# One reduce for both heads' maxima, and broadcast maxima copied into the score banks, in a fused FFN and attention kernel

## The chip, the cores and the metric

The kernel runs on one core of a Trainium2 chip. The metric is the device time of one execution, in microseconds (us), as the median of several runs. Five engines of the core work side by side, each on its own queue in program order: TensorE (PE, with its weight loads PEld), VectorE (DVE), ScalarE (ACT), GpSimd (POOL) and SyncE (SP), which here issues all DMAs.

## The reference

A "macaron" layer on x of shape 4 x 1024 x 128: half an FFN, attention, half an FFN, each on a layer norm of x.

```python
x = x + 0.5 * ffn(layernorm(x))
x = x + attn(layernorm(x))
x = x + 0.5 * ffn(layernorm(x))
```

The FFN is a mixture of 8 experts of width 128 with a router. The attention has 16 heads of 64 dimensions; queries, keys and values come from 64-dimensional latents, queries and keys get a rotary embedding:

```python
scores = jnp.einsum('bhqd,bhkd->bhqk', q, k) * scale      # scale = 1/8
attn = jax.nn.softmax(scores, axis=-1)
out = jnp.einsum('bhqk,bhkd->bhqd', attn, v)
out = out.transpose(0, 2, 1, 3).reshape(b, s, H * DH)
out = out @ w_out.T + residual
```

## The kernel before

The order of all instructions on every engine is written out by hand; there is no scheduler. Lists of closures (`self.at(group, fn, place)`) are run by `run_later(group, place)` at named places of the loop, and `step(...)` takes pieces of background work (layer norms, the latents of the next batch, the second router) as room allows.

The first FFN takes about the first 220 us, the second the last 150. In between, attention runs in 64 units (`for U in range(NUNIT)`). A unit is one batch, one pair of heads and 512 queries (half of the 1024), and it has 8 slots, one for each chunk of 128 keys. The two heads of a pair lie in partitions 0 to 63 and 64 to 127, so the matmuls of the two heads with 64 rows each use different halves of the array. `rows(0)` and `rows(1)` yield each head's matmuls, and the loop zips them, one of each head at a time.

What a unit computes, in TensorE's order:

- **Scores and maxima.** Per slot and head, four matmuls into one PSUM bank (`score`, L938): key by query as high x high, high x low and low x high parts, and a matmul of one row, `one_row` by `maxr`, which adds minus the row maximum of each query. ScalarE then takes the exponential into `p` (L942), and POOL adds the p of the slots into `acc` (L954). The 16 results of a unit go round six banks: four of `psS`, `psC`, `psX`. Among them stand the maxima of a later unit (`passA`): per head and for 128 queries by 512 keys, one matmul of the high parts into that head's bank `psA[hh]` (L912) and at once a VectorE reduce of that bank (L913). There are 8 such steps per head in a unit. `MAXIMA` holds at which positions among the 32 score matmuls of each head six of them stand: 2, 8, 13, 19, 24, 29 for head 0 and 0, 5, 11, 16, 21, 27 for head 1; the last two follow among the side work. `AHEAD = 15` slots lie between a score and the maxima computed beside it.
- **Side work** (`self.halves`): the output projection of an earlier unit (`outp`, L997) into banks `bankO` and the rotary embedding's matmuls (L797) into `rope_banks`, for a later batch.
- **Denominators** of the unit before (`den`, L974): four column sums of `acc` by a matmul with ones, into `psS[3]`, copied out by ScalarE and written to DRAM as `d1`; a transposing load brings them back as `dT` (L982), and VectorE takes the reciprocal for the projection's scaling (L993, L1012).
- **Values** (`values`, L962): 32 matmuls of p with the latent keys into `psC`, then a ScalarE copy to `osb` (L965).

After the side work VectorE has the rotary steps (L810 to L823) and the two additions of the projection to X (L1006), one at place "end" and one at "late".

When the last of a unit's 16 maxima is done, a small reduce (L917) combines them to `m8` [128, 8], negated. `max_row`, at place "mid" of the same unit, writes it to DRAM (`d`) and loads it back transposed into `maxr` as one row per head. All these DMAs stand on SP's queue, in order with the rotary stores (`qs`, `ks`), the latents' loads (`C_l`) and the loads of QT and KT, 16 of them for every two units. A DMA whose data is not ready holds the queue.

Of the kernel before, what the change touches and what calls it, by code (L numbers as in the profile page):

```python
# [10 lines left out]
F32 = mybir.dt.float32  # L11
# [13 lines left out]
LOWER = 0.5 - float(np.log(4.0 / 3.0))  # L25
UPPER = 0.5
CENTER = 1.0 / float(np.e)
AHEAD = 15
NSLOT = B * 128
NGRP = NSLOT // 4  # L30
NUNIT = NSLOT // 8
PBUFS = 10
MAXIMA = ((2, 8, 13, 19, 24, 29), (0, 5, 11, 16, 21, 27))
OTHER, VECTOR, PE, NEVER, SCALAR, POOL = 0, 1, 2, 3, 4, 5
NROPE = 9
ACTS = (4, 6, 7)
SWITCH, HOLD = 49, 49
FAR = 8
WLAG, GS, GD = 4, 17, 22
RATE0, RATE1, RATE2, RATE3 = 0.8, 2.8, 2.6, 1.6  # L40
# [7 lines left out]
class Kernel:  # L48
# [10 lines left out]
    def setup(self):  # L59
# [5 lines left out]
        self.prep = pool("prep", 1)  # L65

        bank = lambda name: pool(name, 1, space=PSUM).tile([128, 512], F32, name=name)
        self.psA, self.psS, self.psC, self.psX = [bank(f"ps_a{i}") for i in range(2)], [bank(f"ps_s{i}") for i in range(4)], bank("psc"), bank("psx")
        self.rest, self.nrest, self.slot, self.bankO = self.psA, 0, -NSLOT, None
        self.rope_banks = self.psA  # L70

# [25 lines left out]
        for t in self.maxr:  # L97
            nc.gpsimd.memset(self.f(t), 0.0)

        self.table = const.tile([128, 3, S], F32, name="table")  # L100
        self.rt = self.prep.tile([128, 4, 512], F32, name="rt")
        self.wr = const.tile([128, 2, 16], F32R, name="wr")
# [798 lines left out]
    def passA(self, a, hh):  # L901

        nc = self.nc
        U, i = divmod(a, 8)
        P, half = divmod(U, 2)
        qb, kk = divmod(i, 2)
        m = self.m_of.setdefault(U, [])
        if not m:
            m += [self.ms.tile([128, 2, 4, 2], F32, name="m"), 0]
        q0 = half * 512 + qb * 128  # L910
        r = slice(64 * hh, 64 * hh + 64)
        nc.tensor.matmul(self.psA[hh], self.QT[P % 3][r, 0, q0:q0 + 128], self.KT[P % 3][r, 0, kk * 512:kk * 512 + 512], start=True, stop=True)  # L912
        nc.vector.tensor_reduce(m[0][:, hh, qb, kk:kk + 1], self.psA[hh], AX.X, ALU.max)  # L913
        m[1] += 1
        if m[1] == 16:
            m8 = self.ms.tile([128, 8], F32R, name="m8")
            nc.vector.tensor_reduce(m8, self.m_of.pop(U)[0].rearrange("p h q k -> p (h q) k"), AX.X, ALU.max, negate=True)  # L917
            self.at(self.group, lambda: self.max_row(U, m8), "mid")

    def max_row(self, U, m):  # L920
        nc = self.nc
        d = self.dram.tile([128, 8], F32, name=f"d3_{U % 4}")
        self.dma(out=d, in_=m)
        self.dma(out=self.maxr[U % 2][0:128:64, :].rearrange("h (q p) -> h q p", p=128), in_=d.rearrange("p (h q) -> h q p", h=2))

    def score(self, s, hh, k):


        nc = self.nc
        U, c = divmod(s, 8)  # L930
        P, half = divmod(U, 2)
        qs = slice(half * 512, half * 512 + 512)
        ks = slice(c * 128, c * 128 + 128)
        r = slice(64 * hh, 64 * hh + 64)
        Q, K = self.QT[P % 3], self.KT[P % 3]
        ps = (self.psS + [self.psC, self.psX])[(2 * (s % 8) + hh) % 6]
        w, x = ((K[r, 0, ks], Q[r, 0, qs]), (K[r, 0, ks], Q[r, 1, qs]), (K[r, 1, ks], Q[r, 0, qs]), (self.one_row[r, :], self.maxr[U % 2][r, :]))[k]
        nc.tensor.matmul(ps, w, x, start=k == 0, stop=k == 3)  # L938
        if k == 3:
            if hh == 0:  # L940
                self.p_of[s] = self.pp.tile([128, 2, 512], F32, name="p")
            nc.scalar.activation(self.p_of[s][:, hh, :], ps, AF.Exp, scale=0.125)  # L942
            if hh == 1:
                self.accumulate(s)

    def accumulate(self, s):
# [20 lines left out]
    def den(self, U):  # L967

        nc = self.nc
        pd = self.psS[3]  # L970
        parts = [self.p_of[8 * U + c] for c in range(8 - direct(U), 8)] + [self.acc_of[U]]
        for k, part in enumerate(parts):
            for n in range(4):
                nc.tensor.matmul(pd[32 * n:32 * n + 32, 0:256], self.ones, part[:, n // 2, 256 * (n % 2):256 * (n % 2) + 256], start=k == 0, stop=k == len(parts) - 1)  # L974
        dsb = self.op1.tile([128, 256], F32, name="dsb")
        nc.scalar.copy(dsb, pd[:, 0:256])
        dT = self.ms.tile([128, 8], F32, name="dT")

        d1 = self.dram.tile([4, 256], F32, name=f"d1_{U % 4}")
        nc.sync.dma_start(out=d1, in_=dsb[0:128:32, :])  # L980
        g = 2 * U + 4
        self.at(g + (U == NUNIT - 1), lambda: nc.sync.dma_start(out=dT, in_=d1.rearrange("(h x) (y p) -> p (h x y)", x=2, p=128)), "mid")  # L982
        self.at(g + (2 if U == NUNIT - 1 else 1), lambda: self.outp(U, self.osb_of.pop(U), dT), "side")

    def outp(self, U, osb, dT):


        nc = self.nc
        P, half = divmod(U, 2)
        b, j = divmod(P, 8)  # L990
        po = self.bankO or self.psA
        rT = self.ms.tile([128, 8], F32, name="rT")
        nc.vector.reciprocal(rT, dT)  # L993

        def mm(i, hh):
            r = slice(64 * hh, 64 * hh + 64)
            nc.tensor.matmul(po[hh][:, i * 128:(i + 1) * 128], osb[r, i * 128:(i + 1) * 128], self.G[r, j, :], start=True, stop=True)  # L997

        for hh in range(2):
            self.halves[hh] += [lambda i=i, hh=hh: mm(i, hh) for i in range(4)]  # L1000

        def add(hh):

            t0 = b * TPB + 4 * half
            x = self.X[:, t0:t0 + 4, :]
            nc.vector.tensor_tensor(x, po[hh].rearrange("p (t d) -> p t d", t=4), x, ALU.add)  # L1006

        def scale():
            for hh in range(2):
                for i in range(4):  # L1010
                    c = slice(i * 128, (i + 1) * 128)
                    nc.scalar.activation(po[hh][:, c], po[hh][:, c], AF.Identity, scale=rT[:, 4 * hh + i:4 * hh + i + 1])  # L1012

        self.at(self.group, scale, "scale")
        self.at(self.group, lambda: add(1))
        self.at(self.group, lambda: add(0), "late")

    def run(self):
        nc, tc = self.nc, self.tc
# [39 lines left out]
        with ExitStack() as ctx:  # L1059
# [20 lines left out]
            def bg1(n, point):  # L1080
# [9 lines left out]
                if point == 2 and n >= 64 - AHEAD:  # L1090
                    self.group = (n - 64) // 4
                    for hh in range(2):
                        self.passA(n - 64 + AHEAD, hh)
                    if n % 4 in (1, 3):
                        self.run_later(self.group, ("mid", "end")[n % 4 // 2])
                if point < 3:
                    return
                if n == FAR:
# [24 lines left out]
        for _ in streams[2].pop() if streams[2] else ():  # L1123
            pass
        assert not (streams[0] or streams[2])
        self.rest, self.rope_banks, self.bankO = [self.psX, self.psS[3]], self.psS[1:3], [self.psX, self.psS[0]]
        flows, needs, blocks = [], {}, list(range(1, B))
        self.attending = True

# [27 lines left out]
        for U in range(NUNIT):  # L1157
# [4 lines left out]

            def rows(hh):
                maxima = lambda i: self.passA(s0 + AHEAD + i, hh) if s0 + AHEAD + i < NSLOT else None
                for n in range(32):
                    if n in MAXIMA[hh]:
                        yield lambda n=n: maxima(MAXIMA[hh].index(n))
                    yield lambda n=n: self.score(s0 + n // 4, hh, n % 4)
                if hh == 1:
                    yield lambda: maxima(6)  # L1170
                for n, fn in enumerate(side[hh]):
                    if hh == 0 and n == 2:
                        yield lambda: maxima(6)
                    yield fn
                if hh == 0 and len(side[hh]) < 3:
                    yield lambda: maxima(6)
                yield lambda: maxima(7)

            for n, pair in enumerate(zip_longest(rows(0), rows(1))):
                for fn in pair:  # L1180
# [2 lines left out]
                if n == 0:  # L1183
                    while self.deferred:
                        self.deferred.pop(0)()
                    for _ in range(2):
                        step(POOL, OTHER)
                if n == 9:
                    self.run_later(2 * U, "mid")
                    rope(U, "high")  # L1190
# [10 lines left out]
                    self.run_later(2 * U, "end")  # L1201
                if n == 26:
                    self.run_later(2 * U + 1, "mid")
                if n == 32:
                    self.run_later(2 * U + 1, "side")
                    rope(U, "side")
            self.halves = [[], []]
# [7 lines left out]
            rope(U, "vector")  # L1215
            self.run_later(2 * U + 1, "end")
            rope(U, "low")
            self.run_later(2 * U + 1, "late")
            rope(U, "end")
            for k in range(8):  # L1220
                self.values(s0 + k)
                if k % 2 == 0 or U < 8:
                    step(SCALAR, OTHER, *((VECTOR,) if k in (2, 3, 6, 7) else ()))
# [13 lines left out]
        with ExitStack() as ctx:  # L1237
# [6 lines left out]
            g = self.ffn_pre(self.prep, (6, 7), x_of, self.wts2[:, 3].rearrange("p e t -> p t e"), rows=3)  # L1244

            def bg2(n):
                for place in ("mid", "side", "scale", "end", "late"):
                    self.run_later(NGRP + 1 + n, place)
                    self.both()
                if n >= GS:  # L1250
# [59 lines left out]
```

## Time and profile before

| | |
|---|---|
| median of 3 runs | 1622.16 us (1620.22 to 1623.82) |
| the profiled execution | 1621.56 us, its profiled span 1619.7 us |
| granted TensorE clock, mean | 0.995 |
| first and last copy of a unit's output (L965) | 240.5 and 1457.4 us, 64 of them |
| DMA | 212.27 MB, 131 GB/s in the mean |

The page of the profile gives the busy time of each engine, a row per resource over 40 equal slices of the span, the chain of work that ended last, and groups of instructions: line, engine, operation, output and inputs by tile, shape, count, then busy time and mean ns of one, then the idle time of the engine just before them and what ended it. Timelines list instructions by start and length, merged where they follow each other. A line of the table of waits gives who waited for whom, the sum in us, how often, and the longest.

TensorE's matmuls are pipelined: the length of one is longer than the distance to the next.

### The profile page before, as it was taken

Reading aid. Unit: us, or ns where it says so; the run is one execution under the profiler, and the core shown is the slowest. Engines: PE = TensorE matmul, PEld = TensorE weight load, DVE = VectorE, ACT = ScalarE, POOL = GpSimd, SP = SyncE. Lnnn points to the kernel's source line nnn. Section 1 sums busy time; section 2 is a strip of 40 time slices with the busy share of each in tenths; the row PEclk is TensorE's granted clock in tenths of the full one; section 3 lists DMA queues with packets and bytes.
Section 4 is the critical chain, followed back from the end, with each engine's and each line's share of the span. In section 5 each row is a group of like instructions: output and inputs, shape, how many; then the busy total and the mean of one; then the engine's idle time right before and its main releaser. Section 6 shows DMA issues by size and latency. Waiting matters only on the chain.

```text
span 1619.7 us, 31073 instructions
## 1 busy us (share of the span) xinstructions
PE 1570.5 (97%) x10924; PEld 1054.0 (65%) x10924; DVE 1298.5 (80%) x2308; ACT 1115.2 (69%) x2488; POOL 1378.8 (85%) x820
## 2 busy tenths in 40 slices
PE   7998999999999999999999999999999999999998
PEld 5876766666666666566666666666666666556776
DVE  6566678898888889988888898889888866616897
ACT  4675667768777777777777777777677676665554
POOL 5678889989888889988989998989998898994676
PEclk9999999999999999999999999999999999999999
DMA  7025565565555555555555555655665532025543
GB/s 230 1 66 157 156 170 144 133 156 132 144 132 131 153 149 138 150 139 138 132 144 144 133 142 135 166 151 139 152 153 137 130 93 55 2 93 148 140 132 102
DMA packets 241148, 212.27 MB, mean 131 GB/s; under 512 B 157664, under 2 KB 170592, under 8 KB 240224
## 3 DMA queue, kind: packets, MB, share of 16 engines
q1 hardware_dynamic: 240992, 210.28, 50.0%
q8 instruction: 87, 1.43, 0.4%
q14 instruction: 69, 0.57, 0.1%
HBM read 130.39 MB, written 79.82 MB: 130 GB/s over the span
## 4 chain that ended last, share of the span: by engine, by line
PE 82%; DVE 6%; ACT 4%; POOL 3%; DMA 2%; issue 2%; SPq 1%; POOLq 0%; DVEq 0%; ACTq 0%
PE psc L962 25%; PE ps_s L938 21%; PE ps_a L912 8%; PE psc L938 4%; PE ps_s L463 3%; PE psx L938 3%; PE ps_s L543 3%; PE ps_s L797 2%; PE ps_s L997 2%; PE ps_s L974 2%; DVE m L913 2%; PE psx L498 2%; PE psc L434 1%; PE psx L997 1%; PE psc L543 1%
## 5 line engine op out<-in xcount | busy, mean ns | idle before, releaser
L954 POOL TENSOR_TENSOR acc<-acc,p 128x1024 f32<-128x1024 f32 x381 | 907.0, 2381 | 29.8
L913 DVE TENSOR_REDUCE m<-ps_a 128x1 f32<-128x512 f32 x1024 | 671.2, 685 | 161.9 <-PE ps_a L912 138.5
L942 ACT ACTIVATE p<-ps_s 128x512 f32<-128x512 f32 x768 | 411.5, 601 | 66.5 <-PE ps_s L938 42.7
L962 PE MATMUL psc<-p,ckn 128*64 128x512 f32 x2048 | 453.6, 595 | 0.0
L938 PE MATMUL ps_s<-QT,KT 64*128 64x512 f32 x2304 | 420.1, 394 | 0.3 <-DVE C_a L718 0.3
L912 PE MATMUL ps_a<-KT,QT 64*128 64x512 f32 x1024 | 390.1, 413 | 7.6 <-DVE m L913 5.8
L962 PEld LDWEIGHTS psc<-p,ckn 128*64 128x64 f32 x2048 | 141.4, 137 | 282.0 <-issue 282.0
L938 PEld LDWEIGHTS ps_s<-QT,KT 64*128 64x128 f32 x2304 | 284.3, 184 | 57.4 <-DVE X L1006 17.0
L954 POOL TENSOR_TENSOR acc<-p 128x1024 f32<-128x1024 f32 x64 | 153.8, 2403 | 86.8 <-ACT p L942 84.5
L912 PEld LDWEIGHTS ps_a<-KT,QT 64*128 64x128 f32 x1024 | 174.1, 184 | 43.4 <-DVE m L913 17.3
L938 PE MATMUL ps_s<-maxr,one_row 64*128 64x512 f32 x768 | 194.5, 392 | 0.0
L820 ACT CAST hi_r<-ps_s 128x512 fp32r<-128x512 f32 x110 | 64.5, 587 | 122.7 <-DVE ps_s L815 119.5
L938 PE MATMUL psx<-QT,KT 64*128 64x512 f32 x384 | 119.1, 390 | 0.0
L965 ACT COPY osb<-psc 128x512 f32<-128x512 f32 x64 | 37.3, 583 | 111.5 <-PE psc L962 111.5
L938 PE MATMUL psc<-QT,KT 64*128 64x512 f32 x384 | 109.2, 390 | 0.0
L938 PEld LDWEIGHTS ps_s<-maxr,one_row 64*128 64x128 f32 x768 | 102.4, 184 | 10.0
L551 POOL TENSOR_TENSOR p<-eo,p 128x512 fp32r<-128x512 f32 x42 | 62.7, 1499 | 41.5 <-ACT p L550 32.6
L1012 ACT ACTIVATE psx<-psx,rT 128x128 f32<-128x128 f32 x248 | 85.2, 344 | 17.5 <-ACT p L942 11.5
L447 POOL TENSOR_TENSOR X<-X,dtmp 128x512 f32<-128x512 f32 x54 | 69.2, 1281 | 31.7 <-ACT dtmp L446 30.6
L1012 ACT ACTIVATE ps_s<-ps_s,rT 128x128 f32<-128x128 f32 x248 | 84.3, 340 | 6.0
L942 ACT ACTIVATE p<-psc 128x512 f32<-128x512 f32 x128 | 77.4, 605 | 6.7 <-PE ps_a L912 3.3
L942 ACT ACTIVATE p<-psx 128x512 f32<-128x512 f32 x128 | 77.9, 608 | 0.0
(268 smaller groups left out, 2664.0 us busy)
## 6 DMA issues: line engine op xcount, KB each, us to landing
C_l<-cs SPq DMA_DIRECT2D x128, 256.0 KB
QT<-qs SPq DMA_DIRECT2D x256, 128.0 KB
KT<-ks SPq DMA_DIRECT2D x256, 128.0 KB
qs<-hi_r SPq DMA_DIRECT2D x32, 512.0 KB
qs<-eo SPq DMA_DIRECT2D x32, 512.0 KB
ks<-hi_r SPq DMA_DIRECT2D x32, 512.0 KB
ks<-eo SPq DMA_DIRECT2D x32, 512.0 KB
rt<-wt SPq DMA_DIRECT2D x52, 256.0 KB
```

What stands on the lines that cost most here:

```text
L447: nc.gpsimd.tensor_tensor(X[:, t:t + 4, :], X[:, t:t + 4, :], tmp, ALU.add)
L463: nc.tensor.matmul(p, w[:, a, e, :], xs[:, c, :], start=k == 0, stop=k == 2)
L543: nc.tensor.matmul(p, w[:, a, e, :], xs[:, c, :], start=k == 0, stop=k == 2)
L551: (nc.gpsimd if m < N - 1 else nc.vector).tensor_tensor(sh[:, 1, :], hp, self.f(sh[:, 0, :]), ALU.subtract)
L820: nc.scalar.copy(w["hi"][:, k, :], w["ps"][k])
L912: nc.tensor.matmul(self.psA[hh], self.QT[P % 3][r, 0, q0:q0 + 128], self.KT[P % 3][r, 0, kk * 512:kk * 512 + 512], start=True, stop=True)
L913: nc.vector.tensor_reduce(m[0][:, hh, qb, kk:kk + 1], self.psA[hh], AX.X, ALU.max)
L938: nc.tensor.matmul(ps, w, x, start=k == 0, stop=k == 3)
L942: nc.scalar.activation(self.p_of[s][:, hh, :], ps, AF.Exp, scale=0.125)
L954: nc.gpsimd.tensor_tensor(acc, self.p_of[s - 1] if c == 1 else acc, self.p_of[s], ALU.add)
L962: nc.tensor.matmul(self.psC[64 * hh:64 * hh + 64, :], self.ckn[b % 2][:, c, :], self.p_of[s][:, hh, :], start=c == 0, stop=c == 7)
L1012: nc.scalar.activation(po[hh][:, c], po[hh][:, c], AF.Identity, scale=rT[:, 4 * hh + i:4 * hh + i + 1])
```

## The change

- **One reduce for both heads.** The two banks of the maxima become one tile of two banks, `psA2`. `passA` of head 0 only issues its matmul. `passA` of head 1 issues its own and then one VectorE reduce over [128, 2, 512], which writes both heads' columns of m. `MAXIMA` is 1, 6, 11, 16, 21, 26 for both heads, so that the two matmuls stand side by side; the last two steps come ahead of the first and the seventh piece of side work. `AHEAD` is 16, `SWITCH` and `HOLD` are 48.
- **Maxima copied into the banks.** For each unit but the first, the row of maxima goes on from `maxr` to DRAM (`d5`) and comes back as a broadcast to all 128 partitions, `maxb` [128, 2, 512]. At the end of the unit before, `fill` copies it by ScalarE into the two banks of the first slot. There the fourth matmul of each head is left out, and the first three accumulate onto what the bank holds. A unit's score list has 31 steps per head in place of 32.
- **Places.** `max_row` puts its DMAs into the next unit: "first" (d), "mid" (maxr), "end" (d5), and "mid" of its second half (the broadcast). The denominators use `psX` and their transposing load stands at "turn", at the end of the unit that stored them. The projection goes to `psS[0:2]` and the rotary embedding to `psS[2:4]`. Both additions to X stand at "end", ahead of the rotary low parts.
- The projection's four matmuls per bank set the start flag on the first alone.

```diff
-AHEAD = 15
+AHEAD = 16
-MAXIMA = ((2, 8, 13, 19, 24, 29), (0, 5, 11, 16, 21, 27))
+MAXIMA = ((1, 6, 11, 16, 21, 26),) * 2
...
+        self.psA2 = pool("ps_a", 1, space=PSUM).tile([128, 2, 512], F32, name="ps_a")
+        self.psA, ... = [self.psA2[:, i, :] for i in range(2)], ...
...
+        self.maxb = const.tile([128, 2, 512], F32, name="maxb")
+        self.filled = set()
...
         nc.tensor.matmul(self.psA[hh], ...)
-        nc.vector.tensor_reduce(m[0][:, hh, qb, kk:kk + 1], self.psA[hh], AX.X, ALU.max)
         m[1] += 1
+        if hh == 0:
+            return
+        nc.vector.tensor_reduce(m[0][:, :, qb, kk:kk + 1], self.psA2, AX.X, ALU.max)
         if m[1] == 16:
...
-            self.at(self.group, lambda: self.max_row(U, m8), "mid")
+            self.max_row(U, m8)
...
     def max_row(self, U, m):
+        g, row = self.group + 1, self.maxr[U % 2]
         d = self.dram.tile([128, 8], F32, name=f"d3_{U % 4}")
+        d5 = self.dram.tile([2, 512], F32, name=f"d5_{U % 4}")
+        self.at(g, lambda: self.dma(out=d, in_=m), "first")
+        self.at(g, lambda: self.dma(out=row[0:128:64, :]..., in_=d...), "mid")
+        if U:
+            self.at(g, lambda: self.dma(out=d5, in_=row[0:128:64, :]))
+            self.at(g + 1, lambda: self.nc.sync.dma_start(out=self.maxb..., in_=d5....to_broadcast([128, 1024])), "mid")
+
+    def bank(self, s, hh):
+        return (self.psS + [self.psC, self.psX])[(2 * (s % 8) + hh) % 6]
+
+    def fill(self, U):
+        for s, hh in ((0, 0), (0, 1)):
+            self.nc.scalar.copy(self.bank(s, hh), self.maxb[:, hh, :])
+            self.filled.add((8 * U + s, hh))
...
+        filled = (s, hh) in self.filled
+        last = 2 if filled else 3
-        nc.tensor.matmul(ps, w, x, start=k == 0, stop=k == 3)
+        nc.tensor.matmul(ps, w, x, start=k == 0 and not filled, stop=k == last, skip_group_check=filled)
...
-        pd = self.psS[3]
+        pd = self.psX
...
-        self.at(g + (U == NUNIT - 1), lambda: nc.sync.dma_start(out=dT, ...), "mid")
+        self.at(g - 1 + (U == NUNIT - 1), lambda: nc.sync.dma_start(out=dT, ...), "turn")
...
-        self.at(self.group, lambda: add(1))
-        self.at(self.group, lambda: add(0), "late")
+        self.at(self.group, lambda: [add(hh) for hh in range(2)])
...
-        ... self.rope_banks, self.bankO = ..., self.psS[1:3], [self.psX, self.psS[0]]
+        ... self.rope_banks, self.bankO = ..., self.psS[2:4], self.psS[0:2]
...
             rope(U, "low")
-            self.run_later(2 * U + 1, "late")
+            if U + 1 < NUNIT:
+                self.fill(U + 1)
             rope(U, "end")
+            self.run_later(2 * U + 1, "turn")
```

## The prediction

> **What bounds the kernel now.** I read the page's busy table, clock row and chain first, then the groups with shapes kept apart, then the TensorE and VectorE timelines of one attention unit, and last the table of waits.
>
> ```profile
> PE 1570.5 (97%) x10924; PEld 1054.0 (65%) x10924; DVE 1298.5 (80%) x2308; ACT 1115.2 (69%) x2488; POOL 1378.8 (85%) x820
> PEclk9999999999999999999999999999999999999999
> PE 82%; DVE 6%; ACT 4%; POOL 3%; DMA 2%; issue 2%; SPq 1%; POOLq 0%; DVEq 0%; ACTq 0%
> ...
> 535.14:546.90 11.76, 11.76 (x112) 9.55 (x111) 9.85 (x17) 10.32 (x21) 9.88 (x5) 1.00 0.38 107
> 1415.34:1432.77 17.43, 17.03 (x127) 10.39 (x123) 3.87 (x8) 11.07 (x27) 16.96 (x8) 1.00 0.14 11
> ```
>
> TensorE is busy for 97% of the span, at full clock, and is 82% of the chain. The last two lines are stretches (length, then the busy time of PE, PEld, DVE, ACT and POOL, the clock, the DMA share, GB/s). In the first, the scores, maxima, projection and denominators of one undisturbed unit, TensorE has no idle time. The second is a whole late unit that has only 2 of the usual 16 maxima matmuls. So whatever TensorE must wait for here is added to the time.
>
> ```profile
> L913 DVE TENSOR_REDUCE m<-ps_a 128x1 f32<-128x512 f32 x1024 | 671.2, 685 | 161.9 <-PE ps_a L912 138.5 <-PE ps_s L938 6.2 <-PE psc L938 5.3
> L912 PE MATMUL ps_a<-KT,QT 64*128 64x512 f32 x1024 | 390.1, 413 | 7.6 <-DVE m L913 5.8 <-DMA KT<-ks 0.9
> L810 DVE TENSOR_TENSOR rt<-ps_s,table 128x1024 f32<-128x1024 f32 x55 | 66.8, 1215 | 0.0
> L812 DVE TENSOR_TENSOR ps_s<-ps_s,table 128x512 f32<-128x512 f32 x55 | 37.9, 689 | 0.0
> L917 DVE TENSOR_REDUCE m<-m 128x8 fp32r<-128x16 f32 x64 | 10.9, 170 | 2.2
> L965 ACT COPY osb<-psc 128x512 f32<-128x512 f32 x64 | 37.3, 583 | 111.5 <-PE psc L962 111.5
> ...
> 537.55 0.39 PE L938 MATMUL psc<-QT,KT 64*128 64x512 f32 x1
> 537.78 0.39 PE L938 MATMUL psc<-QT,KT 64*128 64x512 f32 x1
> 538.01 0.39 PE L938 MATMUL psc<-QT,KT 64*128 64x512 f32 x1
> ...
> 1337.80 0.68 DVE L913 TENSOR_REDUCE m<-ps_a 128x1 f32<-128x512 f32 x1
> 1338.53 0.50 PE L912 MATMUL ps_a<-KT,QT 64*128 64x512 f32 x2 [0.37 <-DVE m L913]
> 1339.07 1.29 DVE L913 TENSOR_REDUCE m<-ps_a 128x1 f32<-128x512 f32 x2 [0.59 <-PE ps_a L912]
> ...
> PEld ps_a L912 <- DVE m L913: 17.3, 37, 1.1
> PEld ps_s L938 <- DVE X L1006: 17.0, 21, 0.8
> SPq L57 <- DMA d<-m: 146.1, 64, 4.7
> ```
>
> The groups give the durations. The three score lines are one head's matmuls in a row, 0.23 us apart though each lasts 0.39; the other head's lie between them (at 537.56, 537.78, 538.02). A pair of matmuls, one per head, thus costs TensorE 0.228 us. The next three lines are a complete wait loop that occurs now by chance: a reduce ends at 1338.48, the two maxima matmuls start 0.05 later, last 0.50, and the reduce of their banks starts at 1339.07. The waits say how rare that is: 17.3 us over 37 waits at the weight loads, 5.8 at the matmuls.
>
> Off the timeline I measured each unit from its first score to its first denominator matmul. The mean of the first 61 is 11.36 us (8.85 scores, 2.51 projections and the rest); an undisturbed unit takes 11.19 (535.14 to 546.33).
>
> **The change, part by part.**
>
> *One reduce for both heads.* Per unit, 16 reduces of 512 become 8 of 1024. Bounds for the longer one: 689 to 1215 ns is what doubling costs in L812 and L810, the same engine and source; for reduces the slope between L917 (16 elements, 170) and L913 is 1.038 ns an element, so 685 + 512 x 1.038 = 1217. I take 1.217 us. It spares VectorE 2 x 0.60 (starts 0.60 apart where it runs without a pause) less 1.15, some 0.05 us, and VectorE is not the bound.
>
> What it takes away is the second bank in flight. Today, while one head's bank is read, the other head's is written. In the changed kernel both maxima matmuls stand side by side, and the next two must wait until the one reduce of both banks is over. The loop is 0.05 (release) + 0.50 (a stalled pair) + 0.04 (to the reduce's start) + 1.217 = 1.81 us. Between two pairs there stand 5 score pairs, so TensorE is back after 6 x 0.228 = 1.37 us. It waits 0.44 us at each of six pairs, and everything behind it in its queue waits as well: the next scores, then ScalarE's exponentials, POOL's sums. The eighth pair comes after one maxima pair, 4 projection pairs (about 0.22 each) and 2 rotary pairs, 1.57 us, and waits 0.24.
>
> The stage is then paced by the loop: 0.34 from the first scores to the first maxima (as from 535.14 to 535.48), 7 x 1.81 = 12.69, and 0.34 + 0.23 from the last maxima past one rotary pair to the denominators: 13.60 us. Against 11.36 that is +2.24 if no disturbance remains, against 11.19 +2.41 if those of today remain; I take 2.33, since VectorE's odd jobs still delay some reduces. Units 0 to 61 have maxima: 62 x 2.33 = +144 us. An error of 0.05 us in the loop is 0.35 a unit, 22 us.
>
> The Trainium skill, page "Perfetto Trace Analysis", section "Optimizing Scalar/DVE Operations", gives some 125 ns of access overhead per VectorE instruction on PSUM and recommends larger operations if the engine is saturated: 512 instructions fewer would by that be an estimated 64 us gained, a time near 1558. The trace has VectorE at 80% and waiting 138.5 us for these very matmuls, so it is not saturated. The same page, section "Matmuls", says that independent groups should rotate through PSUM banks so that one's evacuation overlaps the next one's matmuls; this speaks against the change, and the loop at 1338 shows why, but it gives no figure.
>
> *Maxima by a ScalarE fill.* For the first key chunk of units 1 to 63 the row matmul of each head is dropped: one pair, 0.228 us x 63 = 14 us of TensorE. Where the loop paces the stage a shorter queue only lengthens the wait, so I count it only in the two units without maxima: -0.5 us. In its place come two ScalarE copies a unit (as L965, 0.58 each, 1.15 in all), put behind both additions into X and ahead of the values. With T the start of the last maxima pair: reduce over at T+1.76, small reduce, five rotary steps to about T+5.6 (0.60 apart, the first 1.2), additions to T+6.8, fills to T+7.5. TensorE, with 7.09 us of values, reaches the next scores at T+8.2. Margin 0.7 us, so cost 0; ScalarE sits idle 111.5 us / 64 = 1.7 us a unit ahead of L965, which covers the copies. The additions now precede the rotary low parts, so the 17.0 us that scores wait for them may go too; I leave that inside the choice of 2.33.
>
> *The DMA chain.* d, maxr, then the row's copy to DRAM and a 512 KB broadcast (63 x 0.5 MB = 33 MB; 131 GB/s at 50% share means about 2 us each at full rate). On SP's queue each link waits for the one before: today's waits for d are 146.1/64 = 2.3 us, 4.7 at worst. Behind the waiting SP stand the rotary stores and the QT and KT loads, which are needed a unit later, and the denominators' store. Four links at the worst 4.7 are 18.8 (the stores and loads between them are issued meanwhile), their own issues 4 x 0.6, and the loads and the transposed load ahead of d some 4: 25 us, against 25.6 from the small reduce to the fill (a unit of 21.2, and T+1.9 to T+6.3). With the mean wait it is 16. I take 0. At the worst no margin is left, so the far end is a fill late by 1 us in each unit, +60 us. The near end is not below 0, since nothing waits for less.
>
> *Denominators, banks, places.* The denominator bank, the transposed load taken a group earlier, the projection in the first two score banks: same instructions, same count. The transposed load follows its store on SP by two loads instead of most of a unit, and so may hold SP for up to 2.3 us, which is among the 4 above. The reciprocal that reads it comes in the next unit, as now. Cost 0, at most a few tenths where a projection waits for the exponential of its new bank: TensorE is waiting for maxima there anyway.
>
> **Sum.** The profiled execution took 1621.56 us (span 1619.7 and 1.9 around it), 0.6 below the median of 1622.16. 1621.6 + 144 - 0.5 = 1765.
>
> The page "TensorE: Matmul & The Clock Gate", section "A second HAM failure mode: psum-queue depth-cycling", has the clock fall to half where TensorE idles briefly between groups; by that the scores of 8.7 us would take an estimated 8 us more a unit, some 500 us in all. The clock here is 1.00 in the late unit too, with TensorE idle 0.4 of 17.43 us, but no row has idle spells every 1.8 us.
>
> **Rivals.**
> 1. *The wait is hidden and the dropped pair counts* (not slower). The loop decides nothing if it is under 1.37 us, that is, if a reduce of 1024 takes less than 0.78 us. Then 63 x 0.228 = 14 us go, and up to 23 + 17 us of today's waits with them: 1568 to 1607, say 1592. For it: today's loop, 0.59 + 0.69 = 1.28, does just fit. Against it: both 1024-element durations above.
> 2. *The fill is late as well* (slower still). The broadcast lands 1 us late per unit on top of the loop: 1765 + 60 = 1825. For it: the chain's worst sum. Against it: longer units give the chain more time.
> 3. *The fill does nothing*, the row matmuls stay. The changed program's TensorE order has them out of the first key chunk, and in looped units the time would be the same 1765.
>
> **How the numbers follow.** Forecast 0.80, rival 1 0.10, rival 2 0.10; rival 3 changes no time. From the loop alone the range is 1735 to 1800 (2.24 to 2.41, 22 us either way for 0.05 us). Up to half the late fill's 60 us belongs inside 8 in 10: 1735 to 1825. A measurement here tells 0.2% from no change. Slower by more: 0.89; within: 0.02 (rival 1 cut down by small losses); faster: 0.09.
>
> **What would show it.** Right: 512 reduces of about 1.22 us; a wait for that reduce of about 0.4 us ahead of most maxima matmuls, 150 to 200 us in all; maxima pairs 1.81 us apart; units of 21 to 22 us; TensorE's share under 93%. Wrong: a reduce near 0.7 us, pairs 1.37 us apart, or long waits of the first scores for ScalarE (rival 2).

## The result, and the profile after

| | before | after |
|---|---|---|
| median of 4 runs each, same chip | 1622.97 us (1620.22 to 1623.82) | 1809.18 us (1806.76 to 1810.03) |
| ratio, 95% interval | | 1.1148 [1.1129, 1.1168] |
| profiled span | 1619.7 us | 1807.3 us |
| granted TensorE clock, mean | 0.995 | 0.988 |
| first product of the values | 233.3 us | 242.2 us |
| from there to the first product of the last unit's values | 1217.0 us | 1395.7 us |
| rest of the span | 169.4 us | 169.5 us |

The last three rows are read off the TensorE timelines; the middle one is what "in attention" means from here on. The 187.6 us between the spans are 8.9 ahead of attention and 178.7 in it. Of all runs below, one of e12 took 2439.57 us at a granted clock of 0.592, against 0.992 to 0.994 in the other three, and is left out of every figure.

The page of after: busy time of the engines, the clock row, and the engines' shares of the chain that ended last.

```profile
PE 1667.4 (92%) x10798; PEld 971.6 (54%) x10798; DVE 1271.1 (70%) x1796; ACT 1187.7 (66%) x2614; POOL 1376.6 (76%) x820
PEclk9998999999999999999999999999999999999999
PE 48%; DVE 36%; ACT 5%; DMA 3%; issue 3%; POOL 3%; SPq 2%; POOLq 0%; DVEq 0%; ACTq 0%
```

VectorE is less busy than before in us and in share (1271.1 against 1298.5), and yet it has gone from 6% of the chain to 36%. TensorE lost 5 points of share. An engine that does less work has become the one that others wait for, so a wait is new, not work.

The groups of after that answer to the maxima's lines, with shapes kept apart, and the copies:

```profile
L919 DVE TENSOR_REDUCE m<-ps_a 128x2 f32<-128x1024 f32 x512 | 627.1, 1225 | 325.8 <-PE ps_a L915 325.3
L915 PE MATMUL ps_a<-KT,QT 64*128 64x512 f32 x1024 | 253.3, 486 | 86.2 <-DVE m L919 82.0 <-DMA KT<-ks 3.1
L915 PEld LDWEIGHTS ps_a<-KT,QT 64*128 64x128 f32 x1024 | 98.0, 185 | 270.9 <-DVE m L919 264.5 <-issue 4.5
L940 ACT COPY ps_s<-maxb 128x512 f32<-128x512 f32 x126 | 74.2, 591 | 21.2 <-DVE X L1026 10.9 <-DMA maxb<-d 9.2
```

Half as many reduces, each 1225 ns instead of 685. The first two lines show both sides waiting: VectorE idles 325.3 us for the maxima matmuls (138.5 before), and TensorE waits for the reduces, 264.5 us at the weight loads and 82.0 at the matmuls (17.3 and 5.8 before). When two engines wait for each other like this, they take turns on one buffer.

The timeline of after, TensorE, PE's weight loads and VectorE, inside one unit's score stage (start, length, instruction, in brackets the idle time before it and what ended it):

```profile
571.62 0.53 PE L915 MATMUL ps_a<-KT,QT 64*128 64x512 f32 x2 [0.16 <-DVE m L919]
573.47 0.50 PE L915 MATMUL ps_a<-KT,QT 64*128 64x512 f32 x2 [0.16 <-DVE m L919]
574.74 0.39 PE L957 MATMUL psc<-QT,KT 64*128 64x512 f32 x1
575.29 0.50 PE L915 MATMUL ps_a<-KT,QT 64*128 64x512 f32 x2 [0.16 <-DVE m L919]
575.63 0.39 PE L957 MATMUL psc<-QT,KT 64*128 64x512 f32 x1
577.11 0.50 PE L915 MATMUL ps_a<-KT,QT 64*128 64x512 f32 x2 [0.18 <-DVE m L919]
...
575.29 0.19 PEld L915 LDWEIGHTS ps_a<-KT,QT 64*128 64x128 f32 x2 [0.59 <-DVE m L919]
...
574.01 1.23 DVE L919 TENSOR_REDUCE m<-ps_a 128x2 f32<-128x1024 f32 x1 [0.60 <-PE ps_a L915]
575.83 1.23 DVE L919 TENSOR_REDUCE m<-ps_a 128x2 f32<-128x1024 f32 x1 [0.59 <-PE ps_a L915]
```

The pairs are 1.85, 1.82 and 1.82 us apart. A reduce ends at 575.24, the pair starts at 575.29, lasts 0.50, and the next reduce starts at 575.83 and takes 1.23. The price of a turn is 0.45 us over the 1.37 that five score pairs and the maxima pair itself take at 0.228 each, but the brackets show only 0.16 of idle time at the matmuls. From the score pair ahead (574.74) to the stalled pair are 0.55 us and from there to the next score pair (575.63) 0.34, where pairs in a run stand 0.23 apart; so 0.32 us go ahead of the stalled pair and 0.11 behind it. The weight load's 0.59 counts from its own early place. None of the bracketed numbers is the cost; the distance between pairs is.

Per unit, from its first product of values to the next unit's, means over 61 units: 19.38 us before, 22.19 after. The score stage (first to last score) took 8.85 and takes 11.01, the side stage (projections and rotary products, up to the denominators) 2.51 and 3.01, the gap ahead of the first score 0.36 and 0.51. In an undisturbed unit it is 18.77 and 21.27.

### The profile page after: what moved, and what is told of

Read it like the earlier page. It is cut to its first block, busy times and chain, and to the rows that moved or that the text cites. A ratio compares the mean times of both kernels' runs of the same rounds, so it can differ in the third digit from the quotient of the medians.

```text
span 1807.3 us, 30594 instructions
## 1 busy us (share of the span) xinstructions
PE 1667.4 (92%) x10798; PEld 971.6 (54%) x10798; DVE 1271.1 (70%) x1796; ACT 1187.7 (66%) x2614; POOL 1376.6 (76%) x820
## 4 chain that ended last, share of the span: by engine, by line
PE 48%; DVE 36%; ACT 5%; DMA 3%; issue 3%; POOL 3%; SPq 2%; POOLq 0%; DVEq 0%; ACTq 0%
DVE m L919 26%; PE psc L982 14%; PE ps_a L915 13%; PE ps_s L466 3%; PE ps_s L546 3%; PE ps_s L1017 3%; PE psx L501 2%; PE ps_s L957 2%; PE ps_s L800 2%; PE psc L437 1%; DVE rt L813 1%; PE psx L994 1%; DVE X L1026 1%; SPq L57 1%; PE psc L546 1%
## 5 line engine op out<-in xcount | busy, mean ns | idle before, releaser
L919 DVE TENSOR_REDUCE m<-ps_a 128x2 f32<-128x1024 f32 x512 | 627.1, 1225 | 325.8 <-PE ps_a L915 325.3
L957 PE MATMUL ps_s<-QT,KT 64*128 64x512 f32 x2304 | 356.1, 402 | 6.1 <-ACT ps_s L940 5.3
L915 PE MATMUL ps_a<-KT,QT 64*128 64x512 f32 x1024 | 253.3, 486 | 86.2 <-DVE m L919 82.0
L957 PEld LDWEIGHTS ps_s<-QT,KT 64*128 64x128 f32 x2304 | 225.3, 188 | 81.4 <-ACT ps_s L940 19.4
L915 PEld LDWEIGHTS ps_a<-KT,QT 64*128 64x128 f32 x1024 | 98.0, 185 | 270.9 <-DVE m L919 264.5
L1032 ACT ACTIVATE ps_s<-ps_s,rT 128x128 f32<-128x128 f32 x496 | 164.3, 341 | 36.8 <-ACT p L962 24.6
L957 PE MATMUL ps_s<-maxr,one_row 64*128 64x512 f32 x642 | 129.0, 393 | 0.0
L1026 DVE TENSOR_TENSOR X<-ps_s,X 128x512 f32<-128x512 f32 x124 | 85.2, 687 | 31.7 <-ACT ps_s L1032 25.5
L940 ACT COPY ps_s<-maxb 128x512 f32<-128x512 f32 x126 | 74.2, 591 | 21.2 <-DVE X L1026 10.9
L957 PEld LDWEIGHTS psc<-QT,KT 64*128 64x128 f32 x384 | 71.7, 187 | 13.7
```

What stands on the lines that cost most here:

```text
L919: nc.vector.tensor_reduce(m[0][:, :, qb, kk:kk + 1], self.psA2, AX.X, ALU.max)
L940: self.nc.scalar.copy(self.bank(s, hh), self.maxb[:, hh, :])
L957: nc.tensor.matmul(ps, w, x, start=k == 0 and not filled, stop=k == last, skip_group_check=filled)
```

## Experiments

Each experiment was timed over three rounds beside the kernel before. Ratios are to it, with 95% intervals.

**The merged reduce: e1 to e3.** Is the loop of pair and reduce the cause, or the copies, the broadcast and the new banks? e1 leaves everything of after but makes the reduce short, which leaves half of the keys out of the maxima:

```
-nc.vector.tensor_reduce(m[0][:, :, qb, kk:kk + 1], self.psA2, AX.X, ALU.max)
+nc.vector.tensor_reduce(m[0][:, :, qb, kk:kk + 1], self.psA2[:, :, 0:256], AX.X, ALU.max)
```

> The changed kernel with one edit: the reduce of both banks reads only the first 256 of the 512 columns of each bank, so half of the keys are left out of the maxima. Loop theory: the reduce falls from 1.23 to about 0.69 us, the loop to 0.05 + 0.50 + 0.04 + 0.69 = 1.28 us, below the 1.37 us that TensorE takes from one pair to the next, so the waits of maxima matmuls for it (346 us in the profile after) fall below 50 and the time to about 1630 (1605 to 1650). Rival, the loss lies in the fill and the DMA chain behind it: the time stays above 1770.

Measured: 1659.26 us, 1.0222 [1.0202, 1.0242]. The groups of e1:

```profile
L919 DVE TENSOR_REDUCE m<-ps_a 128x2 f32<-128x512 f32 x512 | 354.4, 692 | 426.2 <-PE ps_a L915 374.0 <-PE ps_s L800 50.6 <-PE psc L957 1.2
L915 PEld LDWEIGHTS ps_a<-KT,QT 64*128 64x128 f32 x1024 | 110.5, 185 | 47.6 <-DVE m L919 16.0 <-issue 3.6 <-DMA QT<-qs 0.7
```

At 692 ns the loop (some 1.28 us) fits between pairs again. TensorE's weight loads wait 16.0 us instead of 264.5, and 150 of the 186 us are gone. About 36 remain, some 30 more than the loop theory had expected of everything else, and the time lies above its range. That was the first sign of a second cost.

e2 goes the other way: the kernel before with the merged reduce and the new positions, and nothing else of the change.

```
-MAXIMA = ((2, 8, 13, 19, 24, 29), (0, 5, 11, 16, 21, 27))
+MAXIMA = ((1, 6, 11, 16, 21, 26),) * 2
...
-nc.vector.tensor_reduce(m[0][:, hh, qb, kk:kk + 1], self.psA[hh], AX.X, ALU.max)
+if hh == 0:
+    return
+nc.vector.tensor_reduce(m[0][:, :, qb, kk:kk + 1], self.psA2, AX.X, ALU.max)
```

> The kernel before with the reduce alone changed: one tile of two banks, one reduce, both heads' maxima at 1, 6, 11, 16, 21, 26; row matmuls, DMA places, denominators and AHEAD 15 stay. Loop theory: 62 units x 2.5 us more, and a row matmul kept costs nothing in a looped unit, so about 1785 (1765 to 1800). Rival, the fill carries a large part of the loss: about 1700 or less.

Measured: 1777.08 us, 1.0952 [1.0934, 1.0970], as the loop has it: +154 us, 151 of them in attention. The mean unit took 21.85 us, the undisturbed one 21.28, as in after.

e3 keeps after's side-by-side positions but gives each head its own reduce of its own bank again:

```
+nc.vector.tensor_reduce(m[0][:, hh, qb, kk:kk + 1], self.psA[hh], AX.X, ALU.max)
-if hh == 0:
-    return
-nc.vector.tensor_reduce(m[0][:, :, qb, kk:kk + 1], self.psA2, AX.X, ALU.max)
```

> The changed kernel with two reduces of 512 again, one behind each maxima matmul, but both heads' maxima still side by side. Loop theory: head 0's bank is free after 1.28 us, head 1's only after 0.05 + 0.50 + 0.04 + 0.60 + 0.69 = 1.88; a late head 1 leaves room for head 0's reduce in the next round, so rounds of about 1.5 and 1.9 us take turns: 1.65 to 1.7 in the mean, some 1 us a unit less than the changed kernel, about 1740 (1700 to 1790). Rival, only the merged instruction costs: about 1630.

Measured: 1708.94 us, 1.0529 [1.0511, 1.0547]. Two lines of its waits:

```profile
PEld ps_a L914 <- DVE m L915: 119.7, 353, 1.4
PE ps_a L914 <- DVE m L915: 9.2, 17, 0.9
```

The wait at the weight loads is less than half of after's, not gone. So position costs something by itself, 40 us against e4 below, and my 1740 took it for too much. With the reduces apart, the first head's bank is free 0.6 us before the second's. With both matmuls next to each other the second still comes too early.

**Old positions in after: e4.** Two reduces in their staggered places, everything else as in after.

```
-MAXIMA = ((1, 6, 11, 16, 21, 26),) * 2
+MAXIMA = ((2, 8, 13, 19, 24, 29), (0, 5, 11, 16, 21, 27))
```

> The changed kernel with the maxima as before: two reduces, the two heads' positions staggered (2, 8, 13, 19, 24, 29 and 0, 5, 11, 16, 21, 27); fill, DMA chain, denominators and AHEAD 16 stay. Loop theory: no loop decides; the 63 dropped pairs give 14 us, the late fill of the last unit costs 7, ScalarE's background work behind the fills some 9, the start 6: about 1630 (1605 to 1645). Rival, the fill is late in many units: above 1660.

Measured: 1668.86 us, 1.0277 [1.0257, 1.0296]. The rival held: without the loop the rest of the change is not a gain of 14 us but a loss of 46. The waits of e4:

```profile
ACT ps_s L937 <- DMA maxb<-d: 34.7, 18, 9.5
PEld ps_s L954 <- ACT ps_s L937: 32.2, 36, 6.5
PEld psx L709 <- ACT ya L254: 18.4, 20, 4.9
PE psx L709 <- ACT ya L254: 10.5, 4, 4.0
```

Copies wait for the broadcast, 18 times; scores wait for the copies; and the transposes of the next batch's layer norm (L709) wait for ScalarE's norm (L254), part of which stands behind those copies: 18.4 us at the weight loads, against 9.4 in e9 below, which has no copies.

**What the rest consists of: e5 to e8.** e5 is e4 without the two copies (the row matmuls are back, the broadcast is loaded and unused). e6 also leaves out the row's copy to DRAM and the broadcast. e7 is e4 with the copies from a tile set once to a constant, without the chain, so nothing can be late; the first chunk's exponentials are shifted by it. e8 is after, merged, without copies and chain. The cut common to e5, e6 and e8, then that common to e6, e7 and e8:

```
-for s, hh in ((0, 0), (0, 1)):
-    self.nc.scalar.copy(self.bank(s, hh), self.maxb[:, hh, :])
-    self.filled.add((8 * U + s, hh))
+return
...
-if U:
-    self.at(g, lambda: self.dma(out=d5, in_=row[0:128:64, :]))
-    self.at(g + 1, lambda: self.nc.sync.dma_start(out=self.maxb
```

> The staggered kernel with two reduces (46 us over the kernel before) without the two ScalarE copies: all row matmuls are back, the broadcast is still loaded and read by nobody. If the loss lies in copies that wait (for the broadcast, or that hold ScalarE's background work), the time falls to about 1640 (1625 to 1655): 14 us for the row matmuls and 14 for the new banks' waits in the side work are in it, and 5 for the earlier start of the maxima. If the chain on SP's queue itself delays the loads of QT and KT, it stays near 1665.

> As the run before, and the copy of the row to DRAM and the 512 KB broadcast are left out too. What is left of the change is AHEAD 16, the places of the DMAs, the denominators' and the projection's banks. If those are nearly free apart from the start: about 1635 (1620 to 1645), within 5 us of the run before. If the chain holds SP's queue: 15 us or more below the run before.

> The staggered kernel with its two copies, but from a constant of -200 that is set once at the start: no DMA chain, so the copies never wait for a landing (the first chunk's exponentials are shifted by a constant in place of the true maxima). If the late broadcast is the main part of the 46 us: about 1625 to 1635. If ScalarE's order is (background work behind the copies, TensorE waiting for it, the clock halved behind that): 1645 or more, with the four long units of about 23 to 25 us still there.

> The changed kernel with its merged reduce, without copies, copy of the row and broadcast; all row matmuls are back. Loop theory: the row matmuls cost nothing there, so the time falls, by the late fill of the last unit (7 us), the four long units (10) and other waits: about 1785 (1775 to 1795), some 8 over the kernel with the merge alone. If a dropped pair is worth its 0.23 us in a looped unit too, the time stays above 1800.

| | median, us | ratio | mean unit, us | attention, us |
|---|---|---|---|---|
| e4, all but merge and positions | 1668.86 | 1.0277 [1.0257, 1.0296] | 19.99 | 1261.6 |
| e5, no copies | 1636.37 | 1.0076 [1.0060, 1.0093] | 19.60 | 1230.7 |
| e6, no copies, no chain | 1641.29 | 1.0108 [1.0093, 1.0123] | 19.61 | 1230.7 |
| e7, copies of a constant | 1650.03 | 1.0155 [1.0131, 1.0179] | 19.76 | 1239.9 |
| e8, merged, no copies, no chain | 1784.02 | 1.0983 [1.0967, 1.0999] | 21.90 | 1371.0 |

e5 and e6 agree in attention to 0.1 us, so the chain as such costs nothing there by holding SP's queue. Their 5 us lie ahead of attention (first values at 233.5 and 240.2 us), where the builds differ by up to 9 us; I didn't find out what decides that. e7 came out in the range of its second expectation (1645 or more), but the broadcast has its part too: the copies alone cost some 9 us of attention although they remove a score pair per unit, and the late broadcast (e4 over e7) another 22. Its four long units are still there, 22.1 to 23.4 us (22.2 to 24.5 in e4). e8 came out as expected: in after, copies and chain are worth 25 us.

**Why the dropped pair brought nothing: e9 to e12.** Even e6, which has neither loop nor copies, is some 17 us above before, and its stage after the scores takes 2.69 us against 2.51. e9 gives it the old banks back:

```
-pd = self.psX
+pd = self.psS[3]
...
-self.rest, self.rope_banks, self.bankO = [self.psX, self.psS[3]], self.psS[2:4], self.psS[0:2]
+self.rest, self.rope_banks, self.bankO = [self.psX, self.psS[3]], [self.psX, self.psS[2]], self.psS[0:2]
```

> This is e6 (two reduces, old staggered positions, no copies and no broadcast: 1641.3 us) with the three uses of the banks put back as they were before: the rotary embedding works in the two banks that are free then, the projection in the first two, the denominators in the last. Theory (the side stage pays for the banks): in e6 that stage took 0.2 us more per unit than before, since the rotary products now stand behind the unit's last exponentials; put back, the stage returns to about 2.5 us and the time falls by 61 x 0.22 = 13 us, to about 1628 (1620 to 1632). Rival (the stage is longer for the new places of the denominators' DMAs and of the last maxima): it stays at 1637 to 1645.

Measured: 1628.03 us, 1.0031 [1.0020, 1.0043]. The stage is back at 2.46 us. Of the 13 us, 10 are in attention and about 4 again ahead of it.

e10 adds copies to e9, in 31 units only: those whose values loop has no other ScalarE work ahead of them. The broadcast is issued earlier.

```
+if k == 2 and 8 <= U < NUNIT - 2 and not scalars:
+    self.fill(U + 1)
```

> An attempt to beat both kernels: two reduces in their staggered positions, the old banks, and the two copies only in those units (31 of them) whose values loop has no other piece of ScalarE work ahead of the copies, with the broadcast loaded half a unit earlier. Theory (the dropped pair is worth its 0.228 us once neither the copies nor the broadcast come late): 31 x 0.228 = 7 us below e9, so about 1621 if e9 gives 1628 (1610 to 1626). Rival (the copies still hold up the unit's first score products): no lower than e9, with waits of the score products for the copies on the page.

Measured: 1631.95 us, 1.0056 [1.0039, 1.0073]: no lower than e9. It beats after by 177 us and before not at all. The rival's waits are there, 13.7 us in 17 waits of score weight loads for copies, but they are not the whole reason: over ten undisturbed filled units the score stage is 0.235 us shorter than in e9, one pair, as it should be, and the next stage 0.19 longer (2.65 against 2.46). VectorE in one such unit, e9 first and then e10:

```profile
504.52 4.12 DVE L915 TENSOR_REDUCE m<-ps_a 128x1 f32<-128x512 f32 x6 [0.27 <-PE ps_a L914]
508.56 0.19 DVE L1005 RECIPROCAL rT<-dT 128x8 f32<-128x8 f32 x1
508.92 2.69 DVE L915 TENSOR_REDUCE m<-ps_a 128x1 f32<-128x512 f32 x4 [0.16 <-PE ps_a L914]
```

```profile
504.49 4.14 DVE L915 TENSOR_REDUCE m<-ps_a 128x1 f32<-128x512 f32 x6 [0.28 <-PE ps_s L954]
508.55 0.19 DVE L1010 RECIPROCAL rT<-dT 128x8 f32<-128x8 f32 x1
508.90 2.57 DVE L915 TENSOR_REDUCE m<-ps_a 128x1 f32<-128x512 f32 x4 [0.16 <-PE ps_s L954]
```

TensorE ends its scores at 509.36 + 0.43 here and at 509.60 + 0.44 in e9, but VectorE is at the same reduce at the same moment in both: its reduces run almost without a pause from 504.5 to 511.5. TensorE's last maxima matmuls need the banks that these reduces free. The matmuls of e9, then the reduces of e10 one by one and its matmuls:

```profile
509.88 0.39 PE L914 MATMUL ps_a<-KT,QT 64*128 64x512 f32 x1
510.26 0.49 PE L914 MATMUL ps_a<-KT,QT 64*128 64x512 f32 x1
...
508.90 0.69 DVE L915 TENSOR_REDUCE m<-ps_a 128x1 f32<-128x512 f32 x1 [0.16 <-PE ps_s L954]
508.90 1.29 DVE L915 TENSOR_REDUCE m<-ps_a 128x1 f32<-128x512 f32 x2 [0.16 <-PE ps_s L954]
...
509.64 0.50 PE L914 MATMUL ps_a<-KT,QT 64*128 64x512 f32 x1
510.24 0.49 PE L914 MATMUL ps_a<-KT,QT 64*128 64x512 f32 x1
```

In e10 both start 0.05 us after a reduce ends (509.59 and 510.18), the release time of the loop, and the second stands where it stood in e9 (510.26) though the scores ended 0.25 us earlier. So the gain is handed to a wait for VectorE, one that no bracket shows. e11 and e12 are e9 and e10 with reduces of 256 columns:

```
-nc.vector.tensor_reduce(m[0][:, hh, qb, kk:kk + 1], self.psA[hh], AX.X, ALU.max)
+nc.vector.tensor_reduce(m[0][:, hh, qb, kk:kk + 1], self.psA[hh][:, 0:256], AX.X, ALU.max)
```

> e9 (1628.0 us) with maxima taken over 256 of the 512 columns of each bank, which leaves half of the keys out of the maxima. In the profile of e10 the score stage of a filled unit is 0.23 us shorter than the same unit of e9, and its side stage 0.20 us longer (2.65 against 2.45), while VectorE's reduces run back to back there. Theory (VectorE's reduces pace the end of the unit): with shorter reduces the side stage falls by some 0.1 to 0.2 us per unit, so 1616 to 1625. Rival (the side stage is paced by something else, such as ScalarE's exponentials): 1626 to 1630.

> e10 (1632.0 us) with the same shorter reduces, which leave half of the keys out of the maxima; it differs from e11 only in the 31 filled units, their copies and the broadcast. Theory (VectorE takes the dropped pair's gain): now the gain is seen, an undisturbed filled unit is 0.2 us shorter than the same unit of e11, and the whole is level with e11 or up to 7 us below it. Rival (another engine takes the gain): the undisturbed filled units are as long as in e11, and the whole is about 4 us above it, as e10 was above e9.

Measured: 1611.30 us, 0.9924 [0.9909, 0.9939], and 1613.83 us, 0.9949 [0.9929, 0.9969]. Of e11 and then of e12:

```profile
L915 DVE TENSOR_REDUCE m<-ps_a 128x1 f32<-128x256 f32 x1024 | 424.7, 423 | 367.0 <-PE ps_a L914 277.6 <-PE ps_s L949 45.8 <-PE psc L949 23.6
```

```profile
ACT ps_s L937 <- DMA maxb<-d: 28.4, 15, 4.3
```

e11 is 17 us below e9, more than expected, so VectorE's reduces do hold this kernel up, though TensorE looks full. But the gain isn't where the theory had put it: in units 1 to 53 the side stage stays at 2.47 us and the score stage falls from 8.97 to 8.74 in the mean (hardly at all in undisturbed units, 8.69 to 8.68); only in units 54 to 61 does the side stage fall, from 2.45 to 2.06. In e12 twelve undisturbed filled units take 18.41 us where e11 takes 18.63: the pair's 0.22 us is there once VectorE has room, and was 0.05 without (18.72 against 18.77). As a whole e12 missed its expectation, 2.5 us above e11: in five units the broadcast now comes 2.3 to 4.3 us late (the line above has all its waits), and these five alone are some 9 us longer than in e11, while the other 26 are 5 us shorter. Both leave half of the keys out of the maxima, so they are no versions to use.

## Why the prediction was right, and what it mis-sized

The forecast was 1765 us in 1735 to 1825, slower; it took 1809. The mechanism was right, the sum 44 us short. The time lies above the 1800 that the loop alone allowed; it lies in the range because half of a late fill's 60 us was put in. That reserve was meant for a copy late in every unit, while what came was spread otherwise (below), so that it was enough is luck.

*The reduce and the loop.* 1.217 us forecast, 1.225 measured; 0.05, 0.50 and 0.04 forecast, 0.05, 0.50 and 0.04 measured; the loop 1.81 and 1.82. The slope between two reduces (170 ns for 16 elements, 685 for 512) was a better base than the other doubling, 689 ns.

*The stage.* 13.60 us forecast, 13.68 in after's undisturbed units (10.64 + 3.04). The single waits that I listed, six of 0.44 us and one of 0.24, come to 2.88 a unit and don't agree with the 2.41 by which the stage was to grow; it grew by 2.49, so the stage was the better count, and where the rest went was not looked at. For the mean unit I took 2.33, between 2.24 (today's disturbances vanish in the waits) and 2.41 (all stay). That halving was wrong. In e2 the mean unit grew by 2.47 us and the undisturbed one by 2.51: the disturbances of before stay, and the loop comes on top. The loop term was 144 us by the sum and 154 in e2.

*Copies and chain, cost 0.* This is the term that failed: 25 us (after over e8). The margin of 0.7 us was right for an undisturbed unit, which takes 21.27 us with the copies and without. I had worked out one ordinary unit and multiplied. The cost lies in the others. Comparing after with e8 in attention: 7.4 us in the last unit, 9.0 in the four units where the next batch's layer norm on ScalarE stands behind the copies, and some 8 spread over the rest, whose cause stays open. In those four the 1.7 us of idle ScalarE that were to cover the copies, a mean over all units, were not free. The far end of +60, a microsecond in every unit, had the place wrong too: in after a copy waits for the broadcast in the last unit alone (9.2 us is all that the L940 line above has). The last unit, on SP, ScalarE and TensorE of after, and the stretch in which its chain stood still (length, busy time of PE, PEld, DVE, ACT and POOL, the clock, DMA share, GB/s):

```profile
1611.90 0.51 SPq L57 DMA_DIRECT2D d<-maxr  x1
1621.24 0.31 SPq L933 DMA_DIRECT2D maxb<-d  x1
...
1624.64 1.11 ACT L940 COPY ps_s<-maxb 128x512 f32<-128x512 f32 x2 [9.20 <-DMA maxb<-d]
...
1625.28 3.44 PE L957 MATMUL ps_s<-QT,KT 64*128 64x512 f32 x12 [5.28 <-ACT ps_s L940]
...
1612.00:1621.30 9.30, 8.01 (x46) 2.59 (x44) 1.39 (x2) 3.14 (x10) 8.99 (x5) 1.00 0.88 362
```

The two links of the chain stand 9.3 us apart on SP, which waits 8.7 us for the first to land, where I had taken 4.7 as the worst. Four loads for the second FFN, 3.5 MB, were issued just ahead of it, and 362 GB/s over 9.3 us is 3.4 MB; that the small copy lands late behind them is read from this and was not tried by itself. ScalarE waits 9.20 us, TensorE 5.28.

*Denominators, banks, places, cost 0.* 7 us (e8 over e2; 5 when each is held against its own runs of before), of which only 3 lie in attention. My cover, that TensorE waits for maxima there anyway, held for most of it. e6 and e9 show the price of the banks without the cover: 10 us in attention.

*The dropped pair.* −0.5 us forecast since a shorter queue only lengthens the wait; e8 confirms it, with the pair back and the undisturbed unit the same 21.27. That it is worth nearly nothing in e10 as well I had not seen: I read TensorE's 11.76 busy of 11.76 us as the only bound, though a VectorE at 9.85 of the same 11.76 has its pauses in the wrong places.

*The start.* 8.9 us ahead of the first values, 4.4 of them within unit 0 from its first score on, had no term; the lead of the maxima and the switch points moved there. They are partly in the terms above: e2 has 3.1 of them, e8 8.3. What decides them stays open. In attention alone the sum closes: 151 us for the loop, 3 for banks and places, 25 for copies and chain, of 178.7.

*The rivals.* Rival 1 (hidden, 1592) fell with the reduce's 1225 ns. Rival 2 (the copies late in every unit) did not happen as such: the broadcast was late once, and the 25 us lie in a few units. Rival 3 changed no time: e8 has the row matmuls back.

*What would show it.* TensorE's share of 92% and the distances were as forecast. "About 0.4 us ahead of most maxima matmuls, 150 to 200 us in all" reads as 0.16 on the matmul and 0.59 on the weight load, 82.0 and 264.5 us in all: I had given the cost by distance (0.45 us at six pairs in 62 units is 167 us) for a number that the page doesn't print. Units of "21 to 22" were 22.19 in the mean.

## What to carry to other kernels

Merging two consumers into one instruction also merges their buffers. Before merging, work out the round trip (release, refill, start, the longer read) and compare it with the producer's time between refills: 1.82 against 1.37 us cost 154 us here, to spare an engine that was 80% busy 27 us in all. Price an edit in the odd units too (the first, the last, those with extra work), since a margin of 0.7 us in the ordinary unit was negative in at least five others. And an engine at 97% doesn't prove that one instruction less on it will shorten the time: look at whether the second engine's work runs without a pause at the place where the gain must come out.

## What was not expected of the hardware

One reduce over two banks of 256 columns took 692 ns, as long as one over 512 columns of one bank (687): only the number of elements counts here, not the bank boundary.

In these runs half the clock came behind some long pauses and not behind many short ones. The Trainium skill, page "TensorE: Matmul & The Clock Gate", section "A second HAM failure mode: psum-queue depth-cycling", tells of a kernel whose short idle times between groups kept throttling it. Here pauses of 0.16 us every 1.82 us left the clock at 1.00, while ahead of units 9, 12, 24 and 27, where the layer norm stands behind the copies on ScalarE, a pause of 1.74 or 1.75 us was followed by half the clock for about 3.4 us, and with the last unit's pause of 5.28 us came half the clock for 6.8. In before, between the first values and the last unit's, no pause was as long as 0.9 us, and the clock was never halved. After's TensorE, first, then the stretches around it (length, busy time of PE, PEld, DVE, ACT and POOL, the clock, DMA share, GB/s):

```profile
427.64 2.32 PE L982 MATMUL psc<-p,ckn 128*64 128x512 f32 x10
431.70 1.63 PE L710 MATMUL psx<-ident,ya 128*128 128x128 f32 x4 [1.74 <-ACT ya L255]
...
434.28 2.01 PE L957 MATMUL ps_s<-QT,KT 64*128 64x512 f32 x10
```

```profile
422.87:429.90 7.03, 7.03 (x36) 2.20 (x32) 6.79 (x11) 4.33 (x11) 6.81 (x3) 1.00 0.39 112
432.00:436.00 4.00, 3.89 (x18) 2.72 (x19) 1.23 (x1) 2.68 (x7) 0.00 (x0) 0.57 0.52 103
436.00:440.00 4.00, 3.67 (x32) 2.38 (x29) 2.45 (x2) 3.23 (x7) 2.06 (x1) 1.00 0.50 140
```

TensorE waits 1.74 us for ScalarE's L255, which stands behind the copies. Just after, ten score matmuls take 2.01 us, against 1.32 at full clock in an undisturbed unit, in a stretch with the clock at 0.57; the next stretch is at 1.00 again. So a pause was paid for a second time. Length alone doesn't decide: after's attention has pauses of up to 1.62 us with no drop, and before has one of 1.76 us, at 1528 us, with none; in e1 one of 1.20 us (770.3) was followed by a drop, in e3 one of 2.52 us (483.2) was not. The halved stretches in after's four units start at 432.36, 504.04, 766.87 and 838.55 us, which are 21, 77 and 21 steps of 3.413 us apart, and each lasts one such step: the clock seems to be set on a fixed grid, so where a pause falls on it may count as well. That the pause causes the drop is read from these cases and was not tried by itself.
